# Feed-forward of a transformer kernel: 128-row and 64-row products of four channel tiles put in a set order

## The chip, the cores and the metric

The kernel runs on one core of a Trainium2 chip. The metric is the device time of one launch in microseconds (us). Engines named here: TensorE (PE; its weight loads are shown apart as PEld), VectorE (DVE), ScalarE (ACT), GpSimd (POOL) and SyncE (SP, which issues most DMAs).

## The reference, cut to what matters

Four attention layers follow each other on x of 8 x 256 tokens with 320 channels, in float32. The first two end in a gated feed-forward, and that is what the change touches:

```python
def geglu_ff(x, W1, b1, W2, b2):          # W1: 320 x 2560, W2: 1280 x 320
    h = x @ W1 + b1
    a, g = jnp.split(h, 2, axis=-1)       # 1280 inner channels each
    return a * jax.nn.gelu(g) @ W2 + b2
...
x = x + geglu_ff(layer_norm(x, ln3_g, ln3_b), Wff1, bff1, Wff2, bff2)
```

The second layer does the same with the exact gelu. The other parts are self attention, attention over a context of 120 tokens, layer norms and output projections.

## The kernel before, in words

x stays on the chip, 128 tokens to a tile. A feed-forward is done in four blocks of 512 tokens per layer, so eight blocks in all. `ff_item` (L545) returns the steps of one block:

- `project` (L551): layer norm and transposes (L314) of 512 tokens, two times 256, into `xT` (tile xTf). The 320 channels lie in three chunks: two of 128 rows, and one of 64 rows that is held twice, in rows 0 to 63 and in rows 64 to 127.
- `out` (L557): the 1280 inner channels are NF = 10 tiles of 128. Each tile i needs a gate half (k = 1) and a value half (k = 0), each a 128 x 512 result in a PSUM bank of its own, summed over the three chunks. Four products with 128 rows come first (L564: two halves, two chunks), then two with 64 rows (L568), the gate's in rows 64 to 127 of the array and the value's in rows 0 to 63. A float32 product is two instructions in the trace, each with a weight load of its own, so a tile shows as eight of L564 and four of L568. Then ScalarE makes gelu of the gate (L572, tile gl) and VectorE multiplies it with the value (L573, tile hT). After a `yield` the next tile follows.
- After ten tiles, the second product (helper `mm`, L120: 128 rows, 80 instructions per block) goes through hT and W2, and VectorE adds the result to x (L586).

PSUM has two pools: `ps_f` gives pairs of banks (`pair`, L278, tile pf, three of them) and `ps_a` single banks (`bank`, L281, tile pa, two of them). All parts of the flow share them.

The order of the work: `run_flow` (L609) has 40 items in a row: the four blocks of the first layer, 16 attention items, the four blocks of the second layer, and 16 attention items more. In each step it takes the score maxima of the next item (`tops`), the projection of the item after that, the end of the item before, and the `out` of this item, and calls them in turn, up to each one's next `yield`; one such turn is a round. So blocks 0 and 1 of a layer are woven with transposes only, block 2 with the projections of an attention item (`duo`, L127 with 128 rows and L129 with 64), and block 3 with such projections and with the score products of `max_scores` (L369, 32 rows; each round takes two pairs, which VectorE's maxima of L376 release). At L393 these maxima are transposed through a single bank, copied, and sent by DMA (L397) into qT, which L414 of the next item reads. The instructions of each engine are then set in an order at compile time: by the order in the program, but one whose operands or buffers are not yet there is passed over by later ones that are ready. [...]

Of the kernel before, what the change touches and what calls it, by code (L numbers as in the profile page):

```python
# [14 lines left out]
ALU = mybir.AluOpType  # L15
# [3 lines left out]
P = 128  # L19
# [5 lines left out]
NF = FF // P  # L25
# [29 lines left out]
class Kernel:  # L55
# [61 lines left out]
    def mm(self, out, pairs):  # L117

        for i, (l, r) in enumerate(pairs):
            self.nc.tensor.matmul(out, l, r, start=i == 0, stop=i == len(pairs) - 1)  # L120
# [424 lines left out]
    def ff_item(self, blk, ln, which, func, w, brow):  # L545
        nc = self.nc
        (w1, w1c), w2 = w
        b1 = COL_B1 + 2 * NF * which
        it = {}

        def project():  # L551
            it["x"] = xT = self.hp.tile([P, 3, TB], F32, tag="qT", name="xTf", bufs=3)
            for i in range(TB // N):
                self.normed_T(blk * (TB // N) + i, xT, i * N, ln)
                yield

        def out():  # L557
            xT = it["x"]
            hT = [self.hp.tile([P, 4, 512], F32, tag="big", name="hT", bufs=4) for _ in range(3)]
            for i in range(NF):  # L560
                s = self.pair()
                for k, col in ((1, (NF + i) * P), (0, i * P)):
                    for c in range(2):
                        nc.tensor.matmul(s[:, k, :], w1[:, c, col : col + P], xT[:, c, :], start=c == 0, stop=False)  # L564

                for k in (1, 0):
                    r = 64 * k
                    nc.tensor.matmul(  # L568
                        s[:, k, :], w1c[r : r + 64, i * P : (i + 1) * P], xT[r : r + 64, 2, :], start=False, stop=True
                    )  # L570
                gl = self.work.tile([P, TB], F32, tag="gl", name="gl")
                nc.scalar.activation(gl, s[:, 1, :], func, bias=self.cols[:, b1 + NF + i : b1 + NF + i + 1])  # L572
                nc.vector.scalar_tensor_tensor(  # L573
                    hT[i // 4][:, i % 4, :], s[:, 0, :], self.cols[:, b1 + i : b1 + i + 1], gl, ALU.add, ALU.mult
                )
                yield
            for t0 in range(0, TB // P, TPB):
                j = blk * (TB // P) + t0
                x = self.x[:, j : j + TPB, :]
                xb = self.work.tile([P, TPB, C], F32, tag="xb", name="xb", bufs=1)  # L580
                nc.gpsimd.tensor_tensor(xb, x, brow.unsqueeze(1).to_broadcast([P, TPB, C]), ALU.add)  # L581
                po = self.pair()
                for t in range(TPB):
                    o = (t0 + t) * P
                    self.mm(po[:, t, :C], [(hT[i // 4][:, i % 4, o : o + P], w2[:, i, :]) for i in range(NF)])
                nc.vector.tensor_tensor(x, po[:, :, :C], xb, ALU.add)  # L586
                yield

        return lambda: iter(()), project, out, lambda: iter(())

    def weave(self, *parts):
# [525 lines left out]
class Quant:  # L1117
# [134 lines left out]
    def whole(self, b, fast=False):  # L1252

        k, nc, sc, nk = self.k, self.k.nc, self.sc, self.nk
        to = nc.vector if fast else nc.gpsimd
        q, kt = self.q[b], self.kk[b]
        tk = k.work.tile([P, 3 * N], F32, tag="xT", name="tk")
        nc.gpsimd.tensor_scalar(tk[:, : 3 * nk], kt, sc[:, 7:8], MAGIC, ALU.mult, ALU.add)  # L1260
        yield
        tq = k.work.tile([P, 3 * N], F32, tag="xh", name="tq")
        to.tensor_scalar(tq, q, sc[:, 6:7], MAGIC, ALU.mult, ALU.add)
        yield
        kh = self.kk[b] = kt.bitcast(BF16)[:, : 5 * nk].rearrange("p (c n) -> p c n", n=nk)
        to.tensor_scalar(
            kh[:, :3].rearrange("p c n -> p (c n)"), tk[:, : 3 * nk], MAGIC, k.half[:, 0:1], ALU.subtract, ALU.mult
        )
        yield
        to.tensor_scalar(  # L1270
            kh[:, 3:].rearrange("p c n -> p (c n)"), tk[:, : 2 * nk], MAGIC, k.half[:, 1:2], ALU.subtract, ALU.mult
        )
        yield
        qh = self.q[b] = q.bitcast(BF16)[:, : 3 * N].rearrange("p (c n) -> p c n", n=N)
        to.tensor_scalar(qh.rearrange("p c n -> p (c n)"), tq, MAGIC, None, ALU.subtract)
# [424 lines left out]
```

## Time and profile before

| | us |
|---|---|
| timed runs | 2279.45, 2291.24, 2304.24 |
| their median | 2291.24 |
| profiled execution, own time | 2282.32 |
| its span, first to last instruction | 2280.5 |
| L564 busy (640 instructions, mean 0.603) | 294.8 |
| L568 busy (320 instructions) | 90.3 |
| L572 busy (80, mean 0.687) | 55.0 |
| L573 busy (80, mean 0.750) | 60.0 |

The eight feed-forward blocks lie between 697 and 1008 us and between 1473 and 1769 us of the span. A row of the timeline gives start, length, engine, line, operation, output and inputs, shapes and count, and in brackets how long the engine had been idle and what ended that. A count in a timeline row gathers neighbours of the same line. Products overlap each other, so the length of a row of products is longer than the distance to the next row's start.

### The profile page before, as it was taken

What the parts mean: (1) busy time and instruction counts of PE and PEld (TensorE: products, weight loads), DVE (VectorE), ACT (ScalarE), POOL (GpSimd) and SP (SyncE); (2) the same over time, 40 slices, a digit from 0 to 9 for tenths busy, and PEclk for the clock granted to TensorE, in tenths of its full rate; (3) what the DMA queues carried; (4) which work ended last, traced back from release to release, by engine and by line L of the source; (5) the groups of instructions that cost most, each with busy time, mean ns of one, the idle gap of its engine ahead of it and who ended that gap; (6) DMA issues with size and microseconds to landing.
All of it is one profiled execution on the core that took longest, in us unless ns stands there. A gap on an engine that the chain in (4) does not pass through costs nothing.

```text
span 2280.5 us, 38243 instructions
## 1 busy us (share of the span) xinstructions
PE 2090.2 (92%) x16413; PEld 1181.9 (52%) x16413; DVE 1116.1 (49%) x1691; ACT 824.9 (36%) x1249; POOL 359.0 (16%) x370
## 2 busy tenths in 40 slices
PE   6978878799899999999999999999999899999997
PEld 4643344454444555455555555444554555566664
DVE  3288675545763221325656567611121466556465
ACT  2337866457643121114444433411101233222221
POOL 1093045450411000000000010100000100000100
PEclk9979888899899999999999999999999899999999
DMA  4010000353111000020000001100000200000000
GB/s 114 9 19 2 2 1 1 101 136 86 43 54 45 0 1 0 1 90 2 2 2 22 27 24 35 46 0 0 1 1 1 67 25 27 17 22 25 25 18 16
DMA packets 79304, 63.23 MB, mean 28 GB/s; under 512 B 48410, under 2 KB 68318, under 8 KB 78622
## 3 DMA queue, kind: packets, MB, share of 16 engines
q1 hardware_dynamic: 75070, 57.06, 8.9%
q10 hardware_dynamic: 4064, 3.71, 0.6%
q8 instruction: 130, 2.13, 0.4%
q14 instruction: 40, 0.33, 0.0%
HBM read 42.61 MB, written 17.37 MB: 26 GB/s over the span
## 4 chain that ended last, share of the span: by engine, by line
PE 73%; DVE 15%; ACT 4%; issue 3%; POOL 2%; SPq 2%; DMA 1%; ACTq 0%; DVEq 0%; POOLq 0%
PE pf L564 13%; PE pf L120 12%; PE pf L127 9%; PE pa L120 6%; PE pa L431 6%; PE pf L414 4%; PE pf L568 4%; PE pf L129 3%; DVE negm L1335 3%; PE pf L1376 2%; DVE rs L439 2%; PE pf L369 2%; PE pa L1398 2%; DVE negm L376 2%; DVE rs L1054 2%
## 5 line engine op out<-in xcount | busy, mean ns | idle before, releaser
L564 PE MATMUL pf<-xTf,ff 128*128 128x512 f32 x640 | 294.8, 603 | 3.5 <-DVE negm L376 2.5
L420 ACT ACTIVATE e<-pf 128x1024 f32<-128x1024 f32 (+2 forms) x176 | 157.7, 944 | 225.0 <-PE pf L414 218.4
L376 DVE TENSOR_REDUCE negm<-pf 128x4 f32<-128x1024 f32 (+4 forms) x224 | 187.8, 885 | 93.0 <-PE pf L369 93.0
L439 DVE RECIPROCAL rs<-pa 128x256 f32<-128x256 f32 x88 | 152.3, 1746 | 150.0 <-PE pa L431 150.0
L573 DVE SCALAR_TENSOR_TENSOR hT<-pf,cols_sb,gl 128x512 f32<-128x512 f32 x80 | 60.0, 750 | 331.2 <-ACT gl L572 331.2
L564 PEld LDWEIGHTS pf<-xTf,ff 128*128 128x128 f32 x640 | 115.1, 190 | 161.6 <-issue 154.9
L461 POOL TENSOR_TENSOR xb<-x_sb,brow 128x640 f32<-128x640 f32 x40 | 61.9, 1548 | 831.2 <-DVE x_sb L467 787.2
L1383 ACT ACTIVATE e<-pf,sc_s 128x1024 f32<-128x1024 f32 x160 | 169.7, 1117 | 51.7 <-PE pf L1376 45.6
L1335 DVE TENSOR_REDUCE negm<-pf 128x4 f32<-128x1024 f32 (+2 forms) x128 | 143.3, 1133 | 65.9 <-PE pf L1332 59.4
L120 PE MATMUL pf<-ff,hT 128*128 128x320 f32 x640 | 174.4, 434 | 0.0
L572 ACT ACTIVATE gl<-pf,cols_sb 128x512 f32<-128x512 f32 x80 | 55.0, 687 | 304.9 <-PE pf L568 304.9
L120 PEld LDWEIGHTS pf<-ff,hT 128*128 128x128 f32 x640 | 120.9, 190 | 55.5 <-issue 6.1
L414 PE MATMUL pf<-qT,kT 32*128 32x256 f32 (+1 forms) x1280 | 128.1, 412 | 17.0 <-DMA qT<-nT 8.6
L369 PE MATMUL pf<-kT,qT 32*128 32x120 f32 (+1 forms) x1920 | 114.3, 331 | 18.1 <-ACT e L420 18.1
L120 PE MATMUL pa<-o,oT 128*128 128x320 f32 x352 | 105.8, 442 | 12.7 <-DVE oT L440 11.6
L369 PEld LDWEIGHTS pf<-kT,qT 32*128 32x128 f32 x1920 | 84.4, 191 | 55.8 <-ACT e L420 28.1
L581 POOL TENSOR_TENSOR xb<-x_sb,brow 128x640 f32<-128x640 f32 x16 | 25.2, 1573 | 559.2 <-DVE x_sb L586 543.5
L431 PE MATMUL pa<-e,v 128*32 128x256 f32 (+1 forms) x1280 | 107.5, 392 | 2.3 <-ACT e L420 1.7
L1376 PE MATMUL pf<-Q,K 32*128 32x256 bf16 (+1 forms) x960 | 87.6, 300 | 23.7 <-DVE negm L1335 13.3
L1491 DVE TENSOR_SCALAR w<-e 128x1024 bf16<-128x1024 f32 (+2 forms) x128 | 86.0, 680 | 44.8 <-ACT e L1383 44.1
L127 PE MATMUL pf<-xT,q 128*128 128x256 f32 x384 | 103.6, 400 | 2.1 <-DVE hT L573 1.9
L414 PEld LDWEIGHTS pf<-qT,kT 32*128 32x128 f32 (+1 forms) x1280 | 72.0, 183 | 64.3 <-issue 32.2
(279 smaller groups left out, 3359.0 us busy)
## 6 DMA issues: line engine op xcount, KB each, us to landing
ff<-in_L_xattn_Wff_dram SPq DMA_DIRECT2D x1, 2560.0 KB
qT<-nT SPq DMA_DIRECT2D x160, 4.0 KB
ff<-in_L_xattn_ff_w_dram SPq DMA_DIRECT2D x1, 2560.0 KB
out_dram<-x_sb SPq DMA_DIRECT2D x16, 160.0 KB
kd_cross<-kst SPq DMA_DIRECT2D x8, 300.0 KB
vd_cross<-vst SPq DMA_DIRECT2D x8, 300.0 KB
vd_both<-vst SPq DMA_DIRECT2D x8, 300.0 KB
kT<-kd_cross SPq DMA_DIRECT2D x8, 300.0 KB
```

Source lines behind the costliest of these rows:

```text
L120: self.nc.tensor.matmul(out, l, r, start=i == 0, stop=i == len(pairs) - 1)
L127: self.nc.tensor.matmul(o, *t[c], start=c == 0, stop=False)
L369: nc.tensor.matmul(s[j // 2][:, j % 2, o : o + nk], qT[r : r + PAD, g, t * P : (t + 1) * P], kT[r : r + PAD, g, :nk], start=True, stop=True,)
L376: nc.vector.tensor_reduce(negm[:, n, 2 * i : 2 * i + 2, g0 : g0 + len(gs), :].rearrange("p j g t -> p j (g t)"), sv[:, :, :, k0:k1], AX.X, ...
L414: nc.tensor.matmul(s[j // 2][:ks, j % 2, o : o + N], kT[r : r + PAD, g, c * ks : (c + 1) * ks], qT[r : r + PAD, g, :], start=True, stop=True,)
L420: nc.scalar.activation(e[:ks, 2 * i : 2 * i + 2, :n], s[i][:ks, :, :n], AF.Exp, scale=scale)
L431: nc.tensor.matmul(o[j * PAD : (j + 1) * PAD, what * N : (what + 1) * N], w, es[g][:ks, j, c * N : (c + 1) * N], start=first and c == 0 an ...
L439: nc.vector.reciprocal(rs, o[:, N:])
L564: nc.tensor.matmul(s[:, k, :], w1[:, c, col : col + P], xT[:, c, :], start=c == 0, stop=False)
L1335: nc.vector.tensor_reduce(negm[:, 2 * h : 2 * h + 2, gs[0] : gs[-1] + 1, :].rearrange("p j g t -> p j (g t)"), s[:, :, : len(gs) * TPB * n ...
L1376: nc.tensor.matmul(s[at // 2][:ks, at % 2, o : o + N], l, m, start=not shift and o == 0, stop=shift and o + N == n, skip_group_check=True,)
L1383: nc.scalar.activation(e[:ks, :, :n], ps[:ks, :, :n], AF.Exp, scale=self.sc[:ks, 9:10])
```

## The change

Only the loop over the ten tiles in `out` is rewritten. Tiles are taken four at a time. The first two of four begin with their products of 128 rows and end on those with 64; the other two begin on their products with 64 rows and end with those of 128. In the order of the program the products of 64 rows of all four thus stand next to each other, and so do those of 128 rows of neighbouring fours; the last group has only two tiles. Tiles 0, 1 and 2 of a group take a pair each, tile 3 takes two single banks. There is still one `yield` for each tile, but at other places. `mm` ties each of these products to the one before it, with an edge that fixes TensorE's order and adds no semaphore. The number of products, their operands' sizes, and the work of ScalarE and VectorE stay as they were.

```diff
--- before.py
+++ after.py
@@ -557,23 +557,62 @@
         def out():
             xT = it["x"]
             hT = [self.hp.tile([P, 4, 512], F32, tag="big", name="hT", bufs=4) for _ in range(3)]
-            for i in range(NF):
-                s = self.pair()
-                for k, col in ((1, (NF + i) * P), (0, i * P)):
+            s = {}
+            last = None
+
+            def mm(*args, **kw):
+                nonlocal last
+                ins = nc.tensor.matmul(*args, **kw)
+                if last is not None:
+                    order = mybir.DependencyInfo(mybir.DependencyClass.NoSync, mybir.DependencyReason.DATA)
+                    self.tc.add_manual_dep(ins.ins, last.name, order, reason="order of the rows' forms")
+                last = ins.ins
+
+            def whole(i, first):
+                for k in (1, 0):
                     for c in range(2):
-                        nc.tensor.matmul(s[:, k, :], w1[:, c, col : col + P], xT[:, c, :], start=c == 0, stop=False)
+                        col = (k * NF + i) * P
+                        mm(
+                            s[i][k], w1[:, c, col : col + P], xT[:, c, :], start=first and c == 0,
+                            stop=not first and c == 1,
+                        )
+
+            def halves(i, first):
 
                 for k in (1, 0):
                     r = 64 * k
-                    nc.tensor.matmul(
-                        s[:, k, :], w1c[r : r + 64, i * P : (i + 1) * P], xT[r : r + 64, 2, :], start=False, stop=True
+                    mm(
+                        s[i][k], w1c[r : r + 64, i * P : (i + 1) * P], xT[r : r + 64, 2, :], start=first,
+                        stop=not first,
                     )
+
+            def gated(i):
                 gl = self.work.tile([P, TB], F32, tag="gl", name="gl")
-                nc.scalar.activation(gl, s[:, 1, :], func, bias=self.cols[:, b1 + NF + i : b1 + NF + i + 1])
+                nc.scalar.activation(gl, s[i][1], func, bias=self.cols[:, b1 + NF + i : b1 + NF + i + 1])
                 nc.vector.scalar_tensor_tensor(
-                    hT[i // 4][:, i % 4, :], s[:, 0, :], self.cols[:, b1 + i : b1 + i + 1], gl, ALU.add, ALU.mult
+                    hT[i // 4][:, i % 4, :], s[i][0], self.cols[:, b1 + i : b1 + i + 1], gl, ALU.add, ALU.mult
                 )
-                yield
+
+
+            for i in range(0, NF, 4):
+                for j in range(i, min(i + 2, NF)):
+                    ps = self.pair()
+                    s[j] = ps[:, 0, :], ps[:, 1, :]
+                    whole(j, True)
+                    yield
+                for j in range(i, min(i + 2, NF)):
+                    halves(j, False)
+                    gated(j)
+                if i + 2 < NF:
+                    ps = self.pair()
+                    s[i + 2] = ps[:, 0, :], ps[:, 1, :]
+                    s[i + 3] = self.bank(), self.bank()
+                    for j in (i + 2, i + 3):
+                        halves(j, True)
+                    for j in (i + 2, i + 3):
+                        whole(j, False)
+                        gated(j)
+                        yield
             for t0 in range(0, TB // P, TPB):
                 j = blk * (TB // P) + t0
                 x = self.x[:, j : j + TPB, :]
```

## The prediction

> **What bounds the kernel now.** I read the page first: busy shares, then the chain of waits.
>
> ```profile
> PE 2090.2 (92%) x16413; PEld 1181.9 (52%) x16413; DVE 1116.1 (49%) x1691; ACT 824.9 (36%) x1249; POOL 359.0 (16%) x370
> PE 73%; DVE 15%; ACT 4%; issue 3%; POOL 2%; SPq 2%; DMA 1%; ACTq 0%; DVEq 0%; POOLq 0%
> PE pf L564 13%; PE pf L120 12%; PE pf L127 9%; PE pa L120 6%; PE pa L431 6%; PE pf L414 4%; PE pf L568 4%; PE pf L129 3%; DVE negm L1335 3%; PE pf L1376 2%; DVE rs L439 2%; PE pf L369 2%; PE pa L1398 2%; DVE negm L376 2%; DVE rs L1054 2%
> ```
>
> TensorE leads, and the lines the change touches (L564 with 128 rows, L568 with 64) hold 17% of the chain. Next, the windows view over the eight feed-forward blocks: 607 us (697 to 1008 and 1473 to 1769), TensorE busy 601.1, granted clock 1.00. ScalarE (102.9) and VectorE (119.7) have slack; what counts there is TensorE's own pace. So I read one tile in the timeline, TensorE's products first, then the weight loads, whose starts are single:
>
> ```profile
> 707.84 3.70 PE L564 MATMUL pf<-xTf,ff 128*128 128x512 f32 x8
> 711.47 1.13 PE L568 MATMUL pf<-xTf,ff1c 64*128 64x512 f32 x4
> 712.53 3.70 PE L564 MATMUL pf<-xTf,ff 128*128 128x512 f32 x8
> ...
> 710.09 0.19 PEld L564 LDWEIGHTS pf<-xTf,ff 128*128 128x128 f32 x1 [0.24 <-issue]
> 710.52 0.19 PEld L564 LDWEIGHTS pf<-xTf,ff 128*128 128x128 f32 x1 [0.24 <-issue]
> 711.47 0.30 PEld L568 LDWEIGHTS pf<-xTf,ff1c 64*128 64x128 f32 x4 [0.76 <-issue]
> 712.53 0.30 PEld L564 LDWEIGHTS pf<-xTf,ff 128*128 128x128 f32 x2 [0.76 <-issue]
> ```
>
> A tile takes 712.53 - 707.84 = 4.69 us. Inside a form the loads follow at 0.43 (708.38 to 710.52 is five steps: 0.428), with 0.24 idle before each; where the form changes, the idle time is 0.76. The eight wide products are eight such slots; the four 64-row ones go two at a time in the two halves of the array, two slots. Ten slots are 4.28; the other 0.41 is **two changes of form, 0.20 us each**. No semaphore is named at them, only "issue".
>
> [...]
>
> **The change, part by part.**
>
> Number of products, loads, ScalarE and VectorE instructions: unchanged, no DMA moved. Only TensorE's order and the lifetime of the PSUM tiles differ.
>
> *Changes of form removed.* In a block alone (blocks 0, 1 and the first two of the second layer) ten tiles had 20. Now the order is W0 W1 H0-3 W2 W3 W4 W5 H4-7 W6 to W9 H8 H9 (W wide, H half): 6, so 14 fewer. Transposes (L314) and L120 have 128 rows and add none. Blocks 2 (of each layer) carry head projections (L127 wide, L129 half): going through the rounds, 28 become 12 in the first, where four lie between the tiles, and 24 become 8 in the second, with two; 16 fewer each, as H0-3 joins L129 directly. Blocks 3 also carry the score products of L369 (32 rows), a form of their own each round: 33 become 21 and 27 become 13. Sum: 4 x 14 + 2 x 16 + 12 + 14 = 114, at 0.20: **-22.8 us**. All of it is on TensorE's path. The unknown is whether 16 half products in a row keep two per slot. The nearest row is L1017 in the last layer, eight 64-row products of 256 columns: 2021.92 to 2022.98, 1.06 us. Four slots of 0.215 and one change in and out at 0.20 make 1.06: they keep it. Bounds for the 114: 11 us (only the four lone blocks) to 24.
>
> *gl and hT come later for two tiles in four.* ACT L572 (0.69) and DVE L573 (0.75) of tiles i and i+1 now come together behind eight half slots; nobody waits for them but L120, whose product with tile 8 is its 17th instruction, 16 x 0.27 = 4.3 us in; both tiles are done 0.1 + 2 x 0.69 + 0.75 = 2.3 us after H9. Nothing; if the cover were gone, 2 us x 8.
>
> *PSUM kept longer, lone blocks.* Tiles i and i+1 keep their pairs until L573; the third pair is i+2's and the two single banks i+3's. i+4 wants a pair about 8.5 us after i gave its own back (two of H and two W), the banks return one wide tile plus 1.5 us before they are wanted. No wait. Nothing above, at most one wait of 1.5 us per group (3 x 4 x 1.5 = 18) if I have the lifetimes wrong.
>
> *PSUM in blocks 2.* In round 3 the projection takes the third pair, H0 and H1 run (1.7 us), then H2 wants a pair: that of L127/L129, back after L335 (1.27), or tile 0's, back 0.12 + 0.69 + 0.75 = 1.6 after H0. 0 to 1.5 us; I take 0.7, twice: **+1.4**.
>
> *PSUM in blocks 3.* Already tight here:
>
> ```profile
> 926.43 1.15 PE L369 MATMUL pf<-kT,qT 32*128 32x256 f32 x16
> 926.55 0.69 ACT L572 ACTIVATE gl<-pf,cols_sb 128x512 f32<-128x512 f32 x1 [4.62 <-PE pf L568]
> 927.27 0.75 DVE L573 SCALAR_TENSOR_TENSOR hT<-pf,cols_sb,gl 128x512 f32<-128x512 f32 x1 [3.74 <-ACT gl L572]
> 927.94 2.34 DVE L376 TENSOR_REDUCE negm<-pf 128x4 f32<-128x1024 f32 x2
> 928.07 0.30 PEld L564 LDWEIGHTS pf<-xTf,ff 128*128 128x128 f32 x2 [0.90 <-DVE hT L573]
> ```
>
> L369 takes two pairs, and the next tile starts when L573 gives back the last tile's. After the change that tile still holds its pair, so in round 2 W1 waits for the first L376 (1.15 + 1.17 = 2.3 us after L369 starts, against 928.07 - 926.43 = 1.64 now): +0.7. In round 3 two pairs are kept and L369 finds one: half of it runs, then H0, H1, and the other half waits for tile 0's pair (1.6 after H0, 0.86 of it covered by H1: 0.8), the split adds two changes (0.4), and the projection and H2 behind it wait for the next pairs, each behind one L376 (1.17), part of it covered: about 1.6. Together 3.5 per block: **+7.0** for the two. [...] VectorE's later L376 only delays the transposes of L393, which have five rounds left. Bounds: 0 (TensorE's order is settled at compile time and other ready products step in, as at 1473.40, where six of eight L564 run, then L120 of the heads, then two) to 8 per block.
>
> Sum: -22.8 + 1.4 + 7.0 = **-14.4 us** against the profiled execution (2282.32 with its span of 2280.5). The three timed runs are 2279.45, 2291.24 and 2304.24; the profiled one lies 0.4% below their median. The middle of the four is 2286.8; I set the forecast at 2286.8 - 14 = 2273.
>
> **The rivals.**
>
> *Full gain.* The compile-time order fills the waits in blocks 2 and 3. For: ScalarE and VectorE are 17 to 20% busy there, and W3 sits in single banks, which relieves the pairs. Against: 928.07 above. -22.8: 2264.
>
> *Slower.* The kept pairs choke the heads' scores in blocks 3. The place: L369 from round 3 on. If it is put off to the end of the block, the chain L376, L393, the copy and the DMAs of qT (L397) falls behind L120 and TensorE stands before L414 in the next item; five rounds of 2.34 for L376 are 12 us per block, and with the held rounds (up to 8) and blocks 2 the loss is 2 x 20 + 3 = 43: net +20, 2307 (more with the DMAs' landing, which I left out). It decides above 22.8 us of waits, 10 per block 3. Against: DVE idles 3 to 4 us before every L573, and L414 waits for DMA only 8.6 us in the whole run.
>
> *Not what it says.* The added edges order only these products among themselves; other items' may be set inside the H runs, so that only lone blocks gain: -11, 2276.
>
> **How the numbers follow.** Likeliest case 0.53 (own range 2262 to 2284), full gain 0.27, lone blocks only 0.08, slower 0.12. About 1% is what a measurement of this kernel can tell from no change; the runs before spread 1.1%. Faster by over 1% means below 2268.3: three quarters of the full-gain case (0.20) and a fifth of the likeliest (0.11): 0.31. Slower by over 1% is above 2314: the worse half of the slow case, 0.06. Within: 0.63. The range runs from the full gain on the lowest run, 2279.45 - 23 = 2256, to the mildest slow outcomes and the spread of a median, 2294.
>
> **What would show it.** In a lone block (the second, first L564 at 767.65, L120 at 815.06: 47.4 us) the same stretch takes 44.6; half runs of 16 last 3.6 us to the next form; six idle stretches of 0.76 instead of twenty. In blocks 3, L369 or L564 wait for DVE L376 or L573, about 3 us more each. Wrong if the half runs take over 4 us (they don't pair), if TensorE waits in lone blocks for hT, or if L414 after a block 3 waits for DMA.

## The result and the profile after

| | before | changed |
|---|---|---|
| median of the timed runs, us | 2290.63 (8 runs, 2279.45 to 2304.24) | 2268.7 (8 runs, 2264.26 to 2275.15) |
| ratio to before, 95% interval | | 0.9924 (0.99 to 0.9948) |
| span of the profiled execution, us | 2280.5 | 2271.8 |
| the eight blocks, tile 0's first product to the first L120, sum in us | 421.9 | 405.6 |

The ratio is not that of the two medians (0.9904, inside the interval). The forecast was 2273, with 2256 to 2294 as its range, and a change within 1% as the likeliest case. That range also holds the 2290.63 of before, so what speaks for the forecast's mechanism is not that 2268.7 lies in it but the blocks below. The page of the changed kernel, busy shares and the chain of waits (its lines after the rewritten loop stand 39 higher: L564 and L568 have become L565, where all products of a tile are recorded, L572 is L591, L573 is L592):

```profile
PE 2079.1 (92%) x16413; PEld 1195.1 (53%) x16413; DVE 1119.4 (49%) x1691; ACT 824.6 (36%) x1249; POOL 358.9 (16%) x370
PE 73%; DVE 15%; ACT 4%; issue 3%; POOL 2%; SPq 2%; DMA 1%; ACTq 0%; DVEq 0%; POOLq 0%
PE pf L565 13%; PE pf L120 12%; PE pf L127 9%; PE pa L120 6%; PE pa L431 6%; PE pf L414 4%; PE pf L129 3%; PE pa L565 3%; DVE negm L1374 3%; PE pf L369 3%; PE pf L1415 2%; DVE rs L439 2%; PE pa L1437 2%; DVE negm L376 2%; DVE rs L1093 2%
```

Instruction counts are the same and TensorE leads as before. The page can't show more: the gain is in the distances between its products. The timeline of TensorE in the second block, which carries nothing but transposes:

```profile
780.95 2.85 PE L565 MATMUL pf<-xTf,ff1c 64*128 64x512 f32 x12
783.63 1.02 PE L565 MATMUL pa<-xTf,ff1c 64*128 64x512 f32 x4
784.58 3.70 PE L565 MATMUL pf<-xTf,ff 128*128 128x512 f32 x8
788.12 3.60 PE L565 MATMUL pa<-xTf,ff 128*128 128x512 f32 x8
791.55 7.03 PE L565 MATMUL pf<-xTf,ff 128*128 128x512 f32 x16
798.51 2.85 PE L565 MATMUL pf<-xTf,ff1c 64*128 64x512 f32 x12
```

and its weight loads around the second of these changes of form:

```profile
797.13 0.19 PEld L565 LDWEIGHTS pf<-xTf,ff 128*128 128x128 f32 x1 [0.24 <-issue]
797.56 0.19 PEld L565 LDWEIGHTS pf<-xTf,ff 128*128 128x128 f32 x1 [0.24 <-issue]
798.51 0.30 PEld L565 LDWEIGHTS pf<-xTf,ff1c 64*128 64x128 f32 x4 [0.76 <-issue]
799.05 0.19 PEld L565 LDWEIGHTS pf<-xTf,ff1c 64*128 64x128 f32 x2 [0.23 <-issue]
799.48 0.19 PEld L565 LDWEIGHTS pf<-xTf,ff1c 64*128 64x128 f32 x2 [0.23 <-issue]
```

Sixteen half products run from 780.95 to 784.58: 3.63 us, the forecast's 3.6, two to a slot of 0.43 (799.05 to 799.48). Thirty-two wide products follow (784.58 to 798.51) without a stretch of 0.76 in between. The block takes 44.67 us instead of 47.41.

**Block by block**, first product of tile 0 to the first L120, from the timelines, with the changes of form counted along TensorE's order of products. "Again" is a second profiled execution of the changed kernel:

| block | before, us | changed, us | again, us | changes of form |
|---|---|---|---|---|
| 1st layer 0 | 47.51 | 44.77 | 44.77 | 20 to 6 |
| 1 | 47.41 | 44.67 | 44.67 | 20 to 6 |
| 2 | 58.17 | 55.03 | 55.03 | 28 to 12 |
| 3 | 64.37 | 65.25 | 63.56 | 32 to 22 |
| 2nd layer 0 | 50.64 | 47.90 | 47.90 | 20 to 6 |
| 1 | 47.41 | 44.67 | 44.67 | 20 to 6 |
| 2 | 51.65 | 49.51 | 49.50 | 24 to 8 |
| 3 | 54.75 | 53.82 | 53.83 | 26 to 15 |
| sum | 421.9 | 405.6 | 403.9 | 190 to 81 |

The two profiled spans differ by 8.7 us only, though the blocks gave 16.3. The rest is ahead of them: the first product of block 0 starts at 697.85 before and at 706.27 after, and up to there TensorE's order is the same in both kernels, but for neighbours that run side by side (22 of 5359 places). The windows view from 430 to 530 us shows TensorE's granted clock (after the counts) in the first row for before and in the second for the changed kernel:

```profile
430.00:530.00 100.00, 86.42 (x715) 48.54 (x715) 47.69 (x85) 53.66 (x124) 48.37 (x41) 0.93 0.52 143
```

```profile
430.00:530.00 100.00, 86.17 (x630) 47.98 (x628) 45.52 (x75) 48.82 (x116) 48.15 (x41) 0.85 0.49 137
```

At 0.85 instead of 0.93, TensorE got through 630 products in the stretch, not 715. In the profiled executions of this study that start lies anywhere from 695.8 to 707.2 us, whatever the loop does much later. So single spans are off by up to 11 us here, and the experiments below are read from the blocks first.

### The profile page after: what moved, and what is told of

The parts are those of the page before. It is cut to its first block, busy times and chain, and to the rows that moved or that the text cites. A ratio compares the mean times of both kernels' runs of the same rounds, so it can differ in the third digit from the quotient of the medians.

```text
span 2271.8 us, 38259 instructions
## 1 busy us (share of the span) xinstructions
PE 2079.1 (92%) x16413; PEld 1195.1 (53%) x16413; DVE 1119.4 (49%) x1691; ACT 824.6 (36%) x1249; POOL 358.9 (16%) x370
## 4 chain that ended last, share of the span: by engine, by line
PE 73%; DVE 15%; ACT 4%; issue 3%; POOL 2%; SPq 2%; DMA 1%; ACTq 0%; DVEq 0%; POOLq 0%
PE pf L565 13%; PE pf L120 12%; PE pf L127 9%; PE pa L120 6%; PE pa L431 6%; PE pf L414 4%; PE pf L129 3%; PE pa L565 3%; DVE negm L1374 3%; PE pf L369 3%; PE pf L1415 2%; DVE rs L439 2%; PE pa L1437 2%; DVE negm L376 2%; DVE rs L1093 2%
## 5 line engine op out<-in xcount | busy, mean ns | idle before, releaser
L376 DVE TENSOR_REDUCE negm<-pf 128x4 f32<-128x1024 f32 (+4 forms) x224 | 188.0, 885 | 111.1 <-PE pf L369 111.1
L565 PE MATMUL pf<-xTf,ff 128*128 128x512 f32 x512 | 232.5, 601 | 5.2 <-DVE negm L376 5.2
L120 PE MATMUL pf<-ff,hT 128*128 128x320 f32 x640 | 174.4, 434 | 0.0
L592 DVE SCALAR_TENSOR_TENSOR hT<-pf,cols_sb,gl 128x512 f32<-128x512 f32 x64 | 48.0, 751 | 255.9 <-ACT gl L591 253.7
L565 PEld LDWEIGHTS pf<-xTf,ff 128*128 128x128 f32 x512 | 94.9, 191 | 125.4 <-issue 119.5
L120 PEld LDWEIGHTS pf<-ff,hT 128*128 128x128 f32 x640 | 120.9, 190 | 55.5 <-issue 6.1
L414 PE MATMUL pf<-qT,kT 32*128 32x256 f32 (+1 forms) x1280 | 128.3, 412 | 19.5 <-DMA qT<-nT 11.1
L591 ACT ACTIVATE gl<-pf,cols_sb 128x512 f32<-128x512 f32 x64 | 43.9, 687 | 248.8 <-PE pf L565 248.8
L369 PE MATMUL pf<-kT,qT 32*128 32x120 f32 (+1 forms) x1920 | 114.5, 328 | 18.5 <-ACT e L420 18.2
L120 PE MATMUL pa<-o,oT 128*128 128x320 f32 x352 | 105.8, 442 | 13.0 <-DVE oT L440 12.0
L369 PEld LDWEIGHTS pf<-kT,qT 32*128 32x128 f32 x1920 | 84.1, 189 | 57.6 <-ACT e L420 28.4
L414 PEld LDWEIGHTS pf<-qT,kT 32*128 32x128 f32 (+1 forms) x1280 | 72.6, 183 | 66.8 <-issue 34.9
L127 PE MATMUL pf<-xT,q 128*128 128x256 f32 x384 | 101.4, 393 | 0.4 <-ACT e L420 0.2
```

The lines of the kernel that those rows point to most:

```text
L127: self.nc.tensor.matmul(o, *t[c], start=c == 0, stop=False)
L369: nc.tensor.matmul(s[j // 2][:, j % 2, o : o + nk], qT[r : r + PAD, g, t * P : (t + 1) * P], kT[r : r + PAD, g, :nk], start=True, stop=True,)
L376: nc.vector.tensor_reduce(negm[:, n, 2 * i : 2 * i + 2, g0 : g0 + len(gs), :].rearrange("p j g t -> p j (g t)"), sv[:, :, :, k0:k1], AX.X, ...
L414: nc.tensor.matmul(s[j // 2][:ks, j % 2, o : o + N], kT[r : r + PAD, g, c * ks : (c + 1) * ks], qT[r : r + PAD, g, :], start=True, stop=True,)
L565: ins = nc.tensor.matmul(*args, **kw)
```

## The experiments

Theory: each change of row form on TensorE costs 0.20 us, and the gain is their number, less what blocks 2 and 3 wait for PSUM pairs that tiles keep. Rivals: the set order itself does it; only long half runs do it; the 0.20 belongs to something else that comes once per tile; and the loss in blocks 3 is not the pairs'.

**e1_edges: only the added edges, in the old loop.**

```diff
...
-                        nc.tensor.matmul(s[:, k, :], w1[:, c, col : col + P], xT[:, c, :], start=c == 0, stop=False)
+                        mm(s[:, k, :], w1[:, c, col : col + P], xT[:, c, :], start=c == 0, stop=False)
...
-                    nc.tensor.matmul(
+                    mm(
...
```

> The old loop, tile by tile, with only the added edges that fix TensorE's order. If the changes of form carry the gain, nothing moves: lone blocks 47.4 us from first product to L120 as before, blocks 2 at 58.2 and 51.7, blocks 3 at 64.4 and 54.8, time within 0.5% of before. If the set order itself (or what it does to the other items' order) carries part of the gain, blocks 2 and 3 get shorter by 1 us or more each.

Measured: all eight blocks as before, to 0.01 us (47.41, 58.17, 64.37, 54.75 among them), ratio 0.9999 (0.9974 to 1.0024). The edges alone do nothing.

**e2_twos: groups of two, ten changes of form per lone block.**

```diff
...
+            for i in range(0, NF, 2):
...
+                whole(i, True)
+                halves(i, False)
+                gated(i)
...
+                halves(i + 1, True)
+                yield
+                whole(i + 1, False)
+                gated(i + 1)
+                yield
...
```

> Groups of two instead of four: W0 H0 H1 W1, W2 H2 H3 W3 and so on, 10 changes of form per lone block instead of 20 or 6, and one pair kept at a time. At 0.20 us per change: lone blocks 47.4 - 10 x 0.20 = 45.4 us; all eight blocks 113 changes for 190, -15 us if no new wait appears. If a run of half products has to be long to gain (fixed cost of four tiles open at once), lone blocks stay above 46.5.

Measured: lone block 45.52. The block now ends on a wide product, so L120 enters without a change of form and its stretch falls by another 0.11 (21.64 to 21.53): 2.0 us for ten changes, 0.20 each. The eight blocks together take 13.6 less, 14.4 with the eight L120 stretches, for the 15 expected. Ratio 0.9942 (0.9916 to 0.9967). Half runs of eight gain as much per change as runs of sixteen.

**e6_double: four changes per tile.**

```diff
...
+                for c in range(2):
+                    for k, col in ((1, (NF + i) * P), (0, i * P)):
+                        mm(s[:, k, :], w1[:, c, col : col + P], xT[:, c, :], start=c == 0, stop=False, skip_group_check=True)
+                    for k in (1, 0):
+                        r, n = 64 * k, slice(c * N, (c + 1) * N)
+                        mm(
+                            s[:, k, n], w1c[r : r + 64, i * P : (i + 1) * P], xT[r : r + 64, 2, n], start=False,
...
```

> The old loop with each tile's 64-row products split into two times 256 tokens, one after the first 128-row chunk and one after the second: four changes of form per tile instead of two, the same number of columns streamed, four more weight loads. At 0.20 per change: lone blocks 47.4 + 20 x 0.20 = 51.4 us, all blocks 350 changes for 190, +32 us, 1.014 of before. If the price goes with the tile (its first load, its waits) and not with the change, lone blocks stay at 47.4 to 48.

Measured: lone block 51.44, 4.03 us for twenty changes: 0.20 each. The eight blocks together take 33.9 more for 160 changes, about 1.7 of it a halved clock in the first block 3 (0.67 over the 5.20 us from 942.69), of which a later section tells. Ratio 1.0192 (1.0118 to 1.0266), expected 1.014. The weight loads of its second block:

```profile
792.21 0.19 PEld L564 LDWEIGHTS pf<-xTf,ff 128*128 128x128 f32 x1 [0.24 <-issue]
793.16 0.30 PEld L564 LDWEIGHTS pf<-xTf,ff1c 64*128 64x128 f32 x4 [0.76 <-issue]
793.79 0.30 PEld L564 LDWEIGHTS pf<-xTf,ff 128*128 128x128 f32 x2 [0.33 <-issue]
794.33 0.19 PEld L564 LDWEIGHTS pf<-xTf,ff 128*128 128x128 f32 x1 [0.24 <-issue]
```

From 793.16 to 793.79 two slots of 256 columns (0.43 together) and 0.20 pass. The tile's sums and its ScalarE and VectorE work are those of before. Besides the changes, this kernel adds four weight loads per tile, and by itself it does not tell the two apart; e2_twos does, with the loads of before and the same 0.20.

**e3_wide: no change of form left.**

```diff
-                        s[i][k], w1c[r : r + 64, i * P : (i + 1) * P], xT[r : r + 64, 2, :], start=first,
+                        s[i][k], w1c[:, i * P : (i + 1) * P], xT[:, 2, :], start=first,
```

> The changed kernel with the 64-row products issued over all 128 rows (their sums then hold both halves, so values differ). No change of form is left in a lone block, but each of these products takes its slots alone: 10 tiles x 2 slots x 0.429 = 8.6 us more and 6 x 0.20 = 1.2 less than the 44.7 of the changed kernel: 52.1 us per lone block. If the 0.20 belongs to the first load of a fresh sum, or to the semaphore of the result, and not to the form, 1.2 stays: 53.3. Whole kernel 1.015 to 1.02 of before.

Measured: lone block 52.16, expected 52.1 (53.3 for the rival). Its sums are not those of the reference; it is read for its time alone. Ratio 1.0165 (1.0074 to 1.0257). The loads where the run of ff1c ends and the next sums go on:

```profile
792.42 0.19 PEld L565 LDWEIGHTS pa<-xTf,ff1c 128*128 128x128 f32 x1 [0.24 <-issue]
792.85 0.19 PEld L565 LDWEIGHTS pa<-xTf,ff1c 128*128 128x128 f32 x1 [0.24 <-issue]
793.27 0.19 PEld L565 LDWEIGHTS pf<-xTf,ff 128*128 128x128 f32 x1 [0.24 <-issue]
793.70 0.19 PEld L565 LDWEIGHTS pf<-xTf,ff 128*128 128x128 f32 x1 [0.24 <-issue]
```

The same places in the program, other weights, another bank, and 0.24 of idle throughout: the 0.76 belongs to the form.

**a1_again and e4_yields: what blocks 2 and 3 pay for.** e4_yields moves the places of `yield`, and has six of them per block in the loop over tiles instead of ten:

```diff
                     whole(j, True)
-                    yield
                 for j in range(i, min(i + 2, NF)):
                     halves(j, False)
                     gated(j)
...
                     for j in (i + 2, i + 3):
                         halves(j, True)
+                    yield
```

> The changed kernel again on the same chip as e4_yields, as its yardstick: lone blocks 44.7 us, blocks 2 at 55.0 and 49.5, blocks 3 at 63.5 to 65.3 (1.7 us less where the first tile's clock is not halved) and 53.8; 0.992 of before. If the 8.4 us that the profiled execution lost ahead of the first feed-forward block belong to the change, they come again; if they are that execution's clock, they do not.

> The changed order with the places of yield moved, so that tiles 0 and 1 of a group do not keep their pairs over a round: W0 W1 H0-3, yield, W2, yield, W3, yield. If kept pairs are what blocks 2 and 3 paid for, the blocks 3 go to 62 us (from 64.4 before and 65.3 changed) and 52 us (54.8 before, 53.8 changed), the second block 2 to 48.7 (49.5 changed), lone blocks stay at 44.7: 4 to 6 us less than the changed kernel in all, about 0.990 of before. If the loss in the first block 3 was the halved clock of its first tile (1.7 us in that execution), the blocks 3 stay at 63.5 and 53.8 here, and the time is that of the changed kernel.

TensorE in the first block 3 of a1_again, from round 2 on:

```profile
925.34 1.15 PE L369 MATMUL pf<-kT,qT 32*128 32x256 f32 x16
927.79 3.70 PE L565 MATMUL pf<-xTf,ff 128*128 128x512 f32 x8 [1.31 <-DVE negm L376]
931.43 1.13 PE L369 MATMUL pf<-kT,qT 32*128 32x256 f32 x8
932.49 1.13 PE L565 MATMUL pf<-xTf,ff1c 64*128 64x512 f32 x4
933.88 1.13 PE L369 MATMUL pf<-kT,qT 32*128 32x256 f32 x8 [0.27 <-DVE negm L376]
935.19 1.99 PE L127 MATMUL pf<-xT,q 128*128 128x256 f32 x8 [0.18 <-DVE hT L592]
937.12 0.70 PE L129 MATMUL pf<-xT,q 64*128 64x256 f32 x4
937.65 1.88 PE L565 MATMUL pf<-xTf,ff1c 64*128 64x512 f32 x8
```

W1 starts 2.45 us after L369 and waits for L376, as forecast (2.3); and L369 is split in two halves, as forecast, though around H0 alone and not H0 and H1: the second half gets its pair from the first half's own L376, after 0.27, and L127 gets one from L592, after 0.18. Then H1 to H3 join L129 without a change of form.

With e4_yields (same chip as a1_again; profiled once more as e4_again) blocks 2 take 55.38 and 48.86 us, blocks 3 62.57 and 51.79, lone blocks 44.62; the sum is 400.6, 3.3 less than a1_again with the same count of 81 changes. 109 changes at 0.196 are 21.4, and the blocks give 421.9 - 400.6 = 21.3. Some 1.7 us of the 400.6 are a halved clock in the first tile of the first block 3 (0.81 over the 8.80 us from 911.30), of which the next part tells; the blocks without it gave about 23.0, so some waits of before went as well as the changes. In its first block 3, W1 and H0 to H3 follow W0 without a wait; 0.49 us for L592 and 0.26 for L376 are left. With fewer yields the other items' work also falls into fewer rounds, and no run here separates that from the shorter hold of the pairs. Ratios 0.9895 (0.9861 to 0.9929) for e4_yields and 0.9923 (0.9903 to 0.9944) for a1_again; the intervals overlap, so the order of these two rests on the traces.

The 8.4 us ahead of the first block came again in a1_again (706.44), which its expectation took as the sign that they belong to the change. But the two executions lost them at different places. From 430 to 530 us a1_again had a granted clock of 0.93, like before, and the changed kernel's first profile 0.85; from 610 to 690 us a1_again had 0.83, where that profile had 0.94 and before 0.98. Late starts also come without the new order and early ones with it: e6_double, with the old order of the tiles, starts at 706.71, e4_yields, with the new one, at 695.82. Nor would the timed runs allow for it: 16.3 less 8.4 would be a ratio of 0.9966, outside the interval of 0.99 to 0.9948.

**The 1.7 us between the two executions of the changed kernel.** Windows over tile 0 of the first block 3, the changed kernel first, then a1_again:

```profile
921.50:926.80 5.30, 5.27 (x8) 2.03 (x8) 1.82 (x3) 0.23 (x1) 0.00 (x0) 0.68 0.00 0
```

```profile
921.70:925.30 3.60, 3.60 (x8) 1.44 (x8) 1.79 (x3) 0.20 (x1) 0.00 (x0) 1.00 0.00 0
```

The same eight products took 5.30 us at a mean granted clock of 0.68, and 3.60 at 1.00. Ahead of them TensorE waits 1.9 us for L376 in both, as it did in the kernel before; in a1_again:

```profile
921.70 3.70 PE L565 MATMUL pf<-xTf,ff 128*128 128x512 f32 x8 [1.88 <-DVE negm L376]
```

The next two kernels take that stretch away.

**e8_first_banks and e9_block3_banks: tile 0 in the single banks.**

```diff
-                    ps = self.pair()
-                    s[j] = ps[:, 0, :], ps[:, 1, :]
+                    if j == 0 and blk == 3:
+                        s[j] = self.bank(), self.bank()
+                    else:
+                        ps = self.pair()
+                        s[j] = ps[:, 0, :], ps[:, 1, :]
```

This is e9_block3_banks, on top of e4_yields; e8_first_banks lacks `and blk == 3`.

> e4_yields with tile 0 of each block in the two single banks instead of a pair. In blocks 3 its first product then needs no pair that a maximum (L376) has to give back, and the 1.9 us of idle TensorE ahead of it should fall to 0.5 or less in the first layer (0.6 to 0.1 in the second), seen as a shorter stretch from L369 to L565. If the halved clock of the tile behind it comes from that idle stretch, it does not come here: first block 3 at 60.9 us, the stretch ahead of it 2.2 instead of 3.8. Lone blocks stay at 44.6 to 44.8, since tile 3 gets the banks 1.6 us after the first half product and wants them after 1.7. In all 2 to 4 us less than e4_yields. If the idle stretch is the score maxima's own time and just moves to the next product that wants a pair, block and stretch together stay as in e4_yields.

> e4_yields again on the same chip, as the yardstick for e8_first_banks: lone blocks 44.6, blocks 2 at 55.4 and 48.9, blocks 3 at 60.9 (62.6 with the first tile's clock halved) and 51.8 us; about 0.990 of before.

> e8_first_banks with the single banks for tile 0 in blocks 3 only, so that the second layer's first block does not wait for the banks of the head item's end (L120 into pa, which cost 2 to 4 us there). Blocks 3 and the stretches ahead of them as in e8_first_banks (1.8 + 60.9 and 1.8 + 51.8 us), lone blocks 44.6, the second layer's first block 48.0 with 465.6 ahead of it (467.3 if the clock of the head item's first products differs): 3 to 5 us less than e4_yields in the trace, 0.987 of before. If the gain in blocks 3 is given back by the next item instead, 3 us or more appear in the stretch after the first block 3 here too.

e8_first_banks: the idle stretch is gone (1.79 us from the L369 stretch's start to tile 0, instead of 3.83), the first block 3 takes 60.88, and lone blocks 44.73. But the second layer's first block now waits for banks:

```profile
1469.33 3.18 PE L120 MATMUL pa<-o,oT 128*128 128x320 f32 x6 [1.77 <-DVE oT L440]
1472.30 4.01 PE L565 MATMUL pa<-xTf,ff 128*128 128x512 f32 x8
```

In e4_again six products of tile 0 stood ahead of this L120 and covered its wait for L440; here tile 0 has to come behind it. The stretch between the layers grew from 465.6 to 468.8, of which the block behind it gives back 1.1 (46.94 for 48.04), and 0.9908 (0.988 to 0.9937) can't be told from e4_again's 0.9888 (0.9856 to 0.9921). e9_block3_banks does it in blocks 3 alone:

```profile
918.84 1.15 PE L369 MATMUL pf<-kT,qT 32*128 32x256 f32 x16
919.92 0.88 PE L314 MATMUL pf<-ident,xh 128*128 128x128 f32 x6
920.63 3.60 PE L565 MATMUL pa<-xTf,ff 128*128 128x512 f32 x8
924.07 3.60 PE L565 MATMUL pf<-xTf,ff 128*128 128x512 f32 x8
```

Tile 0 follows the transposes at once and runs at full clock. Blocks 3 take 60.88 and 51.83 us, the stretches ahead of them 1.8, lone blocks 44.62, and the stretch between the layers is 465.6 again. In the trace that is 1.7 less than e4_again in the blocks and 2.8 ahead of blocks 3. Ratio 0.9879 (0.9849 to 0.9909), not separable from e4_again's by time; both lie below the changed kernel's 0.9924, with intervals that overlap its own.

## Why the prediction was right, point by point

- *TensorE bounds the blocks, and a change of form costs 0.20 us*: right. In the changed kernel TensorE is busy for 581.8 of the 588.7 us from 706.27 to 1008.15 and from 1474.33 to 1761.13. The price is 0.196 in the changed kernel (2.74 / 14), 0.20 in e2_twos and in e6_double; e3_wide shows that it goes with the form.
- *114 changes removed, -22.8*: 109 were. The lone blocks and blocks 2 were counted rightly (14 and 16 each). In blocks 3 I forecast 33 to 21 and 27 to 13, and two changes per block for the split of L369 in another term, 110 in all; the trace has 32 to 22 and 26 to 15, with the splits. 109 x 0.196 = 21.4.
- *Half runs of sixteen keep two per slot*: right, 3.63 us for 3.6.
- *Later gl and hT, and the PSUM of lone blocks, cost nothing*: right. A lone block took 44.67 for 44.6.
- *PSUM in blocks 2, 0.7 each*: 16 changes are worth 3.14. The first block 2 gained just that, so it waited for nothing; the second gained 2.15, a wait of about 1.0, and its H2 shows 0.72 of it, waiting for L592. 1.0 together for 1.4.
- *PSUM in blocks 3, 3.5 each*: this is the term that was mis-sized. From a1_again, 10 x 0.196 - 0.81 = 1.15 and 11 x 0.196 - 0.92 = 1.24, so 2.4 of waits. The 7.0 hold 0.8 for the splits' changes, which the trace's counts already have, so 6.2 is what it stands for. Round 2 was right (+0.8); the waits of round 3 were priced at 2.4, as if the second half of L369 waited for tile 0's pair, and the projection and H2 for one L376 each. In the first block 3 that half took the pair that the first half's own L376 gave back, 0.27 us after it was wanted, and stood ahead of H1; the projection waited 0.18 for tile 0's pair, and H2 for nothing.
- *Sum*: forecast -14.4, blocks -18.0 (a1_again) or -16.3 (the profiled execution, with 1.7 of a halved clock). The ratio 0.9924 of 2290.63 is -17.4 us. The forecast's ratio, 2273 to the 2286.8 that it started from, is 0.994. The 3.6 us between -14.4 and -18.0 are the over-priced waits (3.4 measured for 7.6), less 0.6 because the changes gave 21.4 for 22.0. How near the median came to 2273 is partly luck: the base (2286.8, measured as 2290.63) and the gain were too low by about the same amount. The 4 us that are left lie within the spread of the timed runs.
- *The rivals*: the heads' scores weren't put off to the end of the block (L369 comes each round), so "slower" had no ground. The first L414 behind the first block 3 comes 25.6 us after its L120 began, as before; one wait of L414 for qT's DMA, some 62 us behind the second block 3, grew from 8.2 to 11.1 and 10.1 us, but the rest of the kernel from that L120 on took no longer (533.1 before, 532.1 and 531.1). "Not what it says" fell too: no other item's product stands inside a half run of a lone block, and blocks 2 gained; in blocks 3 L369 and L127 do stand between H0 and H1. "Full gain" is what e4_yields reaches, in the sum of the blocks.

## What to carry to other kernels

Count the changes of row form along TensorE's order, price one from the distance between starts in a plain stretch (0.20 us here), and order the products so that like forms meet, across neighbouring results if PSUM has room for open sums. What pays for it is the lifetime of PSUM tiles: where other work is woven in at a `yield`, let no tile keep a bank across it that the others want (e4_yields, with fewer yields besides, took 3.3 us less in the blocks than a1_again). A gain of under 1% is proved in such a kernel by the stretches that were changed, not by one span, which moved by 11 us through parts that were the same.

## What the runs showed of the hardware that was not expected

A wait of 1.9 us can cost more than itself. At the start of the first block 3, nine profiled executions had that idle stretch ahead of tile 0 (before, the changed kernel twice, e1_edges, e2_twos, e3_wide, e4_yields twice, e6_double), and in four of them (the changed kernel once, both of e4_yields, e6_double) the following products started 0.85 us apart instead of 0.43 for some 3.4 us: 1.7 us lost. In the two kernels without the stretch the tile ran at full clock.

The record of the granted clock tells the four from the five. In each trace its changes lie on a grid of 3.41 us. Two such windows of the changed kernel's first profile, then one of a1_again; the first figures are the length and TensorE's busy time, and the clock is the third from the end:

```profile
919.23:922.64 3.41, 1.54 (x7) 0.79 (x6) 3.38 (x8) 2.02 (x4) 1.79 (x2) 1.00 0.02 5
922.64:926.06 3.42, 3.42 (x6) 1.37 (x5) 0.68 (x2) 0.00 (x0) 0.00 (x0) 0.50 0.00 0
```

```profile
920.06:923.47 3.41, 1.77 (x4) 0.87 (x5) 3.41 (x5) 1.83 (x4) 1.14 (x2) 1.00 0.00 0
```

In the four, the whole idle stretch fell into one window; TensorE was busy for 1.53 or 1.54 us of it, and the next window had half the clock. In the five, a boundary cut the stretch, the emptier of its two windows had 1.77 to 2.40 us of busy time, and the clock stayed. Over all eleven traces, each of the 114 full-clock windows with less than 1.54 us of busy time was followed by one at half clock, and none of the 5590 with more than 2.9 us was; in between both occur. In the traces of before and of the changed kernel's first execution alone these are 10 of 10 each, none of 515 and of 497, and in between 9 of 86 and 13 of 95. A stretch of 1.88 us at a random place on this grid lies whole in one window in (3.41 - 1.88) / 3.41 = 45% of executions, an estimate; it was four of nine. So the same wait costs 1.9 us or 3.6, and as far as these traces show, where the grid falls decides.
